# An adaLN block with attention and expert FFN on one core: split q, k and V kept in DRAM, later norms early, other work staggered

## The chip, the cores and the metric

The kernel runs on one core of a Trainium2 chip, in one launch. The metric is the device time in microseconds of that launch. Its engines have their own instruction queues: TensorE (PE; PEld is its weight loads), VectorE (DVE), ScalarE (ACT), GpSimd (POOL) and SyncE (SP), which only issues DMAs here.

## The reference

Four batches `x` of 1024 tokens with 256 features go through a modulated attention layer and a modulated FFN:

```python
mod = (_silu(c) @ wmod).reshape(4, 6, 1, -1)
sa, ca, ga, sb, cb, gb = (mod[:, i] for i in range(6))
ga = (2 * (ga >= 0) - 1) * maximum(abs(ga), 0.25)      # gb likewise
h = layernorm(x) * (1 + ca) + sa
x = x + ga * attn(h)          # 16 heads of 16 features, softmax over 1024 keys, projection with bias
h = layernorm(x) * (1 + cb) + sb
x = x + gb * ffn(h)
# ffn, for each batch on its own slices of the 1024 tokens:
base = h @ W_base + b_base
e = relu(h @ W_enc[n] + b_enc[n])                      # 8 autoencoders of width 64
recon = e @ W_dec[n] + b_dec[n]
loss[n] = mean((recon - h) ** 2);  top1 = argmin(loss)
out = base + relu(h @ W_down[top1] + b_down) @ W_up[top1] + b_up
```

All inputs and outputs are float32.

## The kernel before

**Attention.** A batch has four groups of four heads. For each group and each half of 512 queries, the main loop walks over 8 key tiles: 32 (batch, group, half) blocks of 8 steps, 256 steps, two steps to a turn of the loop. `begin` (L534) makes two score tiles `pt` per step on TensorE (L542: k times q, then a matmul that subtracts the row maxima by a mask `pick` and a row tile `mt`), each 128x1024, and ScalarE takes the exponential into `es` (L550). `weigh` (L502) adds the weighted values: four matmuls with `vaug`, V with columns of ones between (L506), so that the row sums come along.

The maxima are wanted before the scores of a group start. So `row_max` (L409) makes the scores once more, in the other orientation (`ps`, L448), a few groups ahead, and VectorE reduces them (L455). Per turn of two steps the loop emits four `pt` and about four `ps` tiles. `pt`, `ps` and the reconstruction tiles `pr` share one PSUM pool, `big`, of three buffers. When a group's maxima are done, `to_row` (L414) turns them on TensorE, copies them on VectorE, splits them on POOL with two instructions (`mrow`, L420 and L421), stores them to DRAM (L423) and loads them back into `mt` (L431).

q and k are split in two float32r parts each (high and low), so that one matmul gives float32 accuracy. `qk_chunk` (L326) makes the q or k of 128 features (two groups) of a batch in four tiles, ScalarE copies, POOL splits (L353, L354) into `qhl` and `khl`, one buffer each, in SBUF. `expand` (L393) copies the rows of two heads from there into 128-row tiles with four DMAs of 128 KB each (L402), two groups ahead. `v_all` (L362) makes V of a batch in four tiles and copies each into four of the five `vaug` buffers (L381): on ScalarE for batch 0, on VectorE later.

**Other work.** Beside the attention of batch b runs the preparation of batch b+1 (norm by `norm_first`, L301, then q, k, v) and `post(b-1)` (L556): projection, second norm, eight encoders in four pairs and two halves, reconstruction and its loss, the choice of the expert, the final matmuls. This work stands in lists, `Stream`s (L837), of items: `X` (instructions off TensorE or DMA), `D` (a TensorE tile with a weight; `FULL` is a whole one, 0.45 a turn of a norm half), `R` (one reconstruction tile, `decode`, L639: `pr` on TensorE, the difference `df` with one buffer on VectorE, L650, two squares with running sums on ScalarE, L655), and the controls `at`, `wait`, `need`, `done`, `take`, `give`, `by`. `fixed(b)` (L997) builds the lists of the preparation, and they start with the batch.

A turn of the loop (L1098) asks which lists are ready and picks a `PATTERN` (L1029) of the letters t (score tile), S (maxima), V (weighted sum), R. With reconstructions at the head of a list it takes two at once. `pressed` (L1114) is true when the sum of the lists' paces exceeds 0.6; then `dense` puts one more D tile in the turn.

**Order.** TensorE's order is that of the program. The other engines' and SyncE's orders come from a scheduler that plays the program with estimated costs; on the chip each engine then takes its instructions in that order. Ahead of the loop stands the prologue: weights, norm of batch 0, q/k of its first chunk, `expand` of two groups, then the maxima of group (0,0), and beside them the transposes of the remaining weights, V of batch 0 and `gate_rows` (L177): five POOL instructions (L192 to L196) and the store `gates` (L197). `post`'s first items, `load` (L560, two loads of x and one of the gates, `gt`) and `gate_proj` (L573, `wpg` and `gpb` on POOL), are ready early too.

A norm half (`norm_items`, L252) is: statistics of four tiles on VectorE (L260, L261), `ve` (L265), `rstd` on POOL (L267), four centrings on POOL (L272), then two turns on TensorE with a ScalarE copy (L284, L285). The tiles of x for it, `xin`, have three buffers, loaded by SyncE (`load_two`, L84); the centred half has the tag `half`, with three buffers shared with the encoders' results.

Of the kernel before, what the change touches and what calls it, by code (L numbers as in the profile page):

```python
# [26 lines left out]
def tile_adaln_block(  # L27
# [111 lines left out]

    def condition():  # L140
# [111 lines left out]
    def norm_items(src_of, dst_of, shift, scale, b, half, name, fast=False):  # L252
# [10 lines left out]
        def spread():  # L263
# [4 lines left out]
            s["xh"] = wa.tile([P, TH, D], F32, tag="half", name=f"xh_{name}", bufs=3)  # L268
# [27 lines left out]
        items += [("D", 0.45, [lambda c=c: turn(c)]) for c in range(NC)] + [("give", "half"), ("wait", 2)]  # L296
        return items
# [3 lines left out]
    def norm_first(b, between=()):  # L301
        def alloc():
            hT_of[b] = wa.tile([P, NC, S], F32, tag="hT", name=f"hT_{b}", bufs=1)

        items = [("X", alloc)]
        for half in range(NH):
            items += norm_items(
                lambda t, half=half: x_in[b, (half * TH + t) // 2][:, t % 2, :],
                lambda: hT_of[b],
                SA,  # L310
                CA,
                b,
                half,
                f"n1_{b}_{half}",
                b == 0,
            )
            if half == 0:
                items += between
        return items
# [6 lines left out]
    def qk_chunk(b, ch):  # L326
        def part(n, which, h, c, s={}):
# [17 lines left out]
            if c == NC - 1:  # L345
# [8 lines left out]
                nc.gpsimd.tensor_tensor(hl[:, 1, hs], fu, hl[:, 0, hs].bitcast(F32), ALU.subtract)  # L354

        return [
            ("D", FULL, [lambda n=n, w=w, h=h, c=c: part(n, w, h, c) for c in range(NC)])
            for n, w in enumerate("qk")
            for h in range(NH)
        ]  # L360

    def v_all(b):  # L362
        def part(u, t, s={}):
# [13 lines left out]
            if t == 1:  # L377
                copy = nc.vector.tensor_copy if b else nc.scalar.copy
                for g in range(NG):
                    va = vaug[(b * NG + g) % NV]  # L380
                    copy(  # L381
                        va[:, 2 * u : 2 * u + 2, :, 0::2],
                        pv[:, :, g * HG * HD : (g + 1) * HG * HD].rearrange(
                            "p t (j e) -> p t j e", e=HD
                        ),
                    )

        return [("D", FULL, [lambda u=u, t=t: part(u, t) for t in range(2)]) for u in range(NT // 2)]
# [4 lines left out]
    def expand(b, g, i):  # L393

        ch, r0 = g // GC, (g % GC) * HG * HD
        for which, order in (("q", (0, 0, 1, 1)), ("k", (0, 1, 0, 1))):
            hl = split[which, b, ch]
            t = wa.tile([P, S], F32R, tag=f"{which}64{i}", name=f"{which}64_{b}_{g}_{i}", bufs=3)
            r = slice(r0 + 2 * i * HD, r0 + (2 * i + 2) * HD)
            for n, part in sorted(enumerate(order), key=lambda x: x[1]):  # L400
                queue = nc.scalar if alone and which == "k" and g == 0 else nc.sync
                queue.dma_start(t[n::4, :].bitcast(F32), hl[r, part, :].bitcast(F32))  # L402
# [153 lines left out]
    def post(b, last=False):  # L556
# [64 lines left out]
        def encode(pr, h, c):  # L621
            hs = slice(h * HALF, (h + 1) * HALF)
            if c == 0:
                s["he", pr, h] = wa.tile([P, HALF], F32, tag="half", name=f"he_{b}_{pr}_{h}", bufs=3)
# [201 lines left out]

    groups = [(b, g) for b in range(B) for g in range(NG)]
# [7 lines left out]
    held = {"half": 3, "centre": 1}  # L835

    class Stream:  # L837
# [3 lines left out]
        def pace(self, step):  # L841

            most, due = 0.0, 0.0
            for item in self.items[self.at :]:
                if item[0] == "D":
                    due += item[1] * len(item[2]) / (2 * FULL)
# [4 lines left out]
            return most  # L851

# [49 lines left out]
    for g in range(2):  # L902
        for i in range(2):
            expand(0, g, i)
    mean_w = cst.tile([P, P], F32, name="mean_w")
# [27 lines left out]
    NV = NG + 1  # L933
# [63 lines left out]
    def fixed(b):  # L997

        moves, work = [], []
        k0 = b * BATCH  # L1000

        def moved(g, i):
            return ("X", lambda: expand(*groups[b * NG + g + 2], i))

        for g in range(NG):
            if b + 1 < B or g < NG - 2:
# [199 lines left out]
```

## Time and profile before

| | us |
|---|---|
| three timed runs: median (lowest, highest) | 1191.78 (1190.69, 1195.03) |
| the profiled execution | 1194.91 |
| its span | 1193.1 |
| mean granted TensorE clock | 0.978 of full |

Busy times by stage of that execution, from windows of the trace:

| stage | from, to (us) | length | PE busy | DVE | ACT | POOL | clock |
|---|---|---|---|---|---|---|---|
| up to the first exponential | 0.24, 80.0 | 79.76 | 46.52 | 42.66 | 13.77 | 26.13 | 0.84 |
| rest of group (0,0) | 80.0, 155.6 | 75.60 | 64.45 | 61.87 | 34.50 | 27.17 | 0.94 |
| rest of batch 0 | 155.6, 323.1 | 167.50 | 160.57 | 125.05 | 106.87 | 19.23 | 1.00 |
| batch 1 | 323.1, 597.8 | 274.70 | 260.31 | 192.59 | 170.77 | 62.27 | 1.00 |
| batch 2 | 597.8, 873.1 | 275.30 | 260.32 | 191.11 | 170.77 | 61.24 | 1.00 |
| batch 3 | 873.1, 1120.8 | 247.70 | 227.84 | 144.08 | 159.98 | 46.38 | 0.99 |
| tail | 1120.8, 1193.1 | 72.30 | 57.84 | 34.57 | 35.68 | 12.34 | 0.90 |

How to read the lines of the profile: "L542 PE MATMUL pt<-q,k" is TensorE's matmul of line 542 that writes pt and reads q and k; "x2048" is a count. In a group's line come busy us and mean ns of one, then the idle time of the engine ahead of these instructions and, after an arrow, the instruction that ended it. In the timeline a line starts with its start and length in us, and the bracket holds the idle time before it and its releaser. A float32 matmul leaves two records. The span's first instruction is at about 0.24 us in these windows.

### The profile page before, as it was taken

Reading aid. Unit: us, or ns where it says so; the run is one execution under the profiler, and the core shown is the slowest. Engines: PE = TensorE matmul, PEld = TensorE weight load, DVE = VectorE, ACT = ScalarE, POOL = GpSimd, SP = SyncE. Lnnn points to the kernel's source line nnn. Section 1 sums busy time; section 2 is a strip of 40 time slices with the busy share of each in tenths; the row PEclk is TensorE's granted clock in tenths of the full one; section 3 lists DMA queues with packets and bytes.
Section 4 is the critical chain, followed back from the end, with each engine's and each line's share of the span. In section 5 each row is a group of like instructions: output and inputs, shape, how many; then the busy total and the mean of one; then the engine's idle time right before and its main releaser. Section 6 shows DMA issues by size and latency. Waiting matters only on the chain.

```text
span 1193.1 us, 16436 instructions
## 1 busy us (share of the span) xinstructions
PE 1077.8 (90%) x6324; PEld 476.5 (40%) x6324; DVE 791.9 (66%) x975; ACT 692.3 (58%) x928; POOL 254.8 (21%) x271
## 2 busy tenths in 40 slices
PE   4768889999999889999999889999999889899995
PEld 3423333434444333345444333345444333344443
DVE  4477977777687666767678666676778777701264
ACT  2114466665666677654556667654655676647662
POOL 3155000200314002240224201140222200042003
PEclk9869999999999999999999999999999999999998
DMA  6522130122121201113131200204040300011001
GB/s 203 142 81 55 41 77 18 50 69 54 44 60 36 61 15 48 54 43 82 38 110 27 56 15 24 64 27 103 17 131 8 76 1 18 15 58 53 18 1 47
DMA packets 42582, 63.92 MB, mean 54 GB/s; under 512 B 13052, under 2 KB 28436, under 8 KB 42504
## 3 DMA queue, kind: packets, MB, share of 16 engines
q1 hardware_dynamic: 40000, 58.41, 18.2%
q10 hardware_dynamic: 1736, 3.15, 0.8%
q0 software_dynamic: 768, 1.31, 0.5%
q8 instruction: 50, 0.82, 0.3%
q14 instruction: 28, 0.23, 0.1%
HBM read 19.39 MB, written 5.19 MB: 21 GB/s over the span
## 4 chain that ended last, share of the span: by engine, by line
PE 69%; ACT 11%; DVE 10%; DMA 4%; issue 4%; POOL 2%; SPq 0%; ACTq 0%; DVEq 0%; POOLq 0%
PE pt L542 18%; PE pv L506 18%; PE ps L448 10%; ACT es L550 6%; DVE mx L455 5%; PE ph L626 4%; PE pr L647 3%; PE pq L338 3%; PE pvp L370 3%; ACT df L655 3%; DVE df L650 3%; PE ppj L591 2%; PE pf L761 2%; PE pk L338 2%; PE ptn_n L284 2%
## 5 line engine op out<-in xcount | busy, mean ns | idle before, releaser
L455 DVE TENSOR_REDUCE mx<-ps 128x2 f32<-128x1024 f32 x512 | 611.8, 1220 | 191.9 <-PE ps L448 188.2
L550 ACT ACTIVATE es<-pt 128x1024 f32<-128x1024 f32 x512 | 510.8, 1022 | 296.2 <-PE pt L542 289.5
L506 PE MATMUL pv<-es,vaug 128*32 128x512 f32 x2048 | 274.6, 607 | 0.1
L448 PE MATMUL ps<-k,q 64*128 64x512 f32 x1024 | 236.4, 461 | 35.0 <-ACT es L550 10.4
L542 PE MATMUL pt<-q,k 64*128 64x512 f32 x1024 | 239.0, 451 | 21.8 <-ACT es L550 10.7
L542 PE MATMUL pt<-mt,pick 64*128 64x512 f32 x1024 | 209.4, 393 | 4.6 <-DMA mt<-mdram 4.6
L448 PEld LDWEIGHTS ps<-k,q 64*128 64x128 f32 x1024 | 98.3, 186 | 201.4 <-issue 92.5
L542 PEld LDWEIGHTS pt<-q,k 64*128 64x128 f32 x1024 | 99.3, 184 | 170.7 <-DVE mx L455 96.8
L655 ACT ACTIVATE df<-df,fbias 128x512 f32<-128x512 f32 x128 | 91.1, 713 | 55.0 <-DVE df L650 55.0
L542 PEld LDWEIGHTS pt<-mt,pick 64*128 64x128 f32 x1024 | 100.4, 186 | 15.6 <-DMA mt<-mdram 5.8
L650 DVE TENSOR_TENSOR df<-pr,h2T 128x1024 f32<-128x1024 f32 x64 | 77.4, 1222 | 42.5 <-PE pr L647 20.7
L506 PEld LDWEIGHTS pv<-es,vaug 128*32 128x32 f32 x2048 | 40.5, 108 | 100.1 <-issue 90.8
L647 PE MATMUL pr<-he,wdec 64*128 64x512 f32 x256 | 64.3, 614 | 6.3 <-ACT es L550 6.2
L484 POOL TENSOR_TENSOR aT<-aT,su 128x512 f32<-128x512 f32 x14 | 17.8, 1273 | 238.9 <-DMA su<-rdram 189.5
L626 PE MATMUL ph<-h2T,wenc 128*128 128x512 f32 x128 | 63.6, 623 | 0.0
L781 DVE TENSOR_TENSOR x<-pf,x 128x512 f32<-128x512 f32 x16 | 10.8, 687 | 54.3 <-PE pf L772 22.1
L353 POOL CAST qhl<-fu_q 128x512 fp32r<-128x512 f32 x14 | 8.5, 610 | 178.4 <-ACT fu_q L352 175.9
L267 POOL TENSOR_TENSOR rstd_n<-ve_n,neghalf 128x4 f32<-128x4 f32 x16 | 16.8, 1048 | 102.2 <-DVE ve_n L265 96.4
L761 PE MATMUL pf<-wbg,h2T 128*128 128x256 f32 x128 | 37.4, 425 | 0.0
L647 PEld LDWEIGHTS pr<-he,wdec 64*128 64x128 f32 x256 | 21.6, 185 | 37.3 <-ACT es L550 13.2
L284 PE MATMUL ptn_n<-ident,xh_n 128*128 128x128 f32 x128 | 23.2, 311 | 14.0 <-ACT h2T L285 6.6
L626 PEld LDWEIGHTS ph<-h2T,wenc 128*128 128x128 f32 x128 | 22.3, 192 | 33.0 <-issue 31.8
(134 smaller groups left out, 755.8 us busy)
## 6 DMA issues: line engine op xcount, KB each, us to landing
q<-qhl SPq DMA_DIRECT2D x128, 128.0 KB
k<-khl SPq DMA_DIRECT2D x120, 128.0 KB
xin<-in_L_attn_x_dram SPq DMA_DIRECT2D x16, 256.0 KB
x<-in_L_attn_x_dram SPq DMA_DIRECT2D x8, 512.0 KB
aT<-ou SPq DMA_DIRECT2D x32, 128.0 KB
out_dram<-x SPq DMA_DIRECT2D x16, 256.0 KB
su<-rdram SPq DMA_DIRECT2D x14, 256.0 KB
wm<-in_L_wmod_dram ACTq DMA_DIRECT2D x1, 1024.0 KB
```

Source lines behind the costliest of these rows:

```text
L284: nc.tensor.transpose(pt[:, t, :], s["xh"][:, t, c * P : (c + 1) * P], ident)
L338: nc.tensor.matmul(pq, wqkv[:, c, n * D + ch * P : n * D + (ch + 1) * P], hT[:, c, hs], start=(c == 0), stop=(c == NC - 1),)
L448: nc.tensor.matmul(ps[:, a, :], q[r, t0 : t0 + P], k[r, h * HALF : (h + 1) * HALF], start=True, stop=True,)
L455: nc.vector.tensor_reduce(mx[:, h, hq, i::2, t], ps, AX.X, ALU.max, negate=True)
L506: nc.tensor.matmul(acc[h][j * STRIP : (j + 1) * STRIP, :], va[:, kt, j, :], es[j // 2][:, j % 2, :], start=(kt == 0), stop=(kt == NT - 1),)
L542: nc.tensor.matmul(pt[:, a, :], k[r, kt * P : (kt + 1) * P] if first else picks[i][r, :], q[r, hs] if first else mt[n % 2][r, hs], start=f ...
L550: nc.scalar.activation(e, pt, AF.Exp, scale=SCALE)
L626: nc.tensor.matmul(s["ph"], wenc[:, c, 2 * pr : 2 * pr + 2, :].rearrange("p n h -> p (n h)"), s["h2T"][:, c, hs], start=(c == 0), stop=(c ...
L647: nc.tensor.matmul(two[:, i, :], wdec[r, pr, c * P : (c + 1) * P], he[r, :], start=True, stop=True)
L650: nc.vector.tensor_tensor(df, two, h2T[:, c, hs].unsqueeze(1).to_broadcast([P, 2, HALF]), ALU.subtract)
L655: nc.scalar.activation(df[:, i, :], df[:, i, :], AF.Square, bias=bdec_of(e, c), accum_out=s["acc"][:, e, c, h : h + 1],)
L761: nc.tensor.matmul(po[u][:, t, :], s["h2T"][:, c, t0 : t0 + P], s["wbg"][:, c, :], start=(c == 0), stop=False,)
```

## The change

- `qk_chunk` stores each finished `qhl` and `khl` to DRAM three steps after its last tile (`hldram`), and `expand` reads from there with two DMAs of 256 KB per tile instead of four of 128 KB; only the first chunk of batch 0 is still read from SBUF. A chunk's tiles wait (`need`) until the other chunk's store has been issued.
- `v_all`: ScalarE copies each V tile into `vo` (one buffer), which is stored to DRAM (`vdram`). Batch 0 also fills `vaug` directly, three groups of it. `vaug` has three buffers instead of five, and `fetch_v` loads a group's values into `vi` and POOL spreads them into `vaug` four steps later.
- The norms of batches 1 to 3 stand in a list of their own from the start of the loop and run as buffers allow; their turns wait until the batch before is through with its q, k and V. `half` has four buffers. q, k and V of batches 1, 2 and 3 have the end steps of `AHEAD`; before, those of batch b+1 were spread over batch b.
- `post`'s six lists end 36, 28, 28, 18, 12 and 0 steps before the end of their batch instead of all at it.
- A turn takes one reconstruction instead of two when no list's `rate` asks for more than one per step.
- Reconstructions count 0.5 in `pace`, and `pressed` begins at 0.75.

```diff
+    hldram, vdram = {}, [dram.tile([P, NT, D], F32, name=f"vdram_{b}") for b in range(B)]
...
-            s["xh"] = wa.tile([P, TH, D], F32, tag="half", name=f"xh_{name}", bufs=3)
+            s["xh"] = wa.tile([P, TH, D], F32, tag="half", name=f"xh_{name}", bufs=4)
...
-    def norm_first(b, between=()):
...
+    def norm_first(b, load=None):
...
+        if b == 0:
+            return [("X", alloc)] + [item for centred, turns in both for item in centred + turns]
+        items = []
+        for half in range(NH):
+            for u in range(half * NT // 4, (half + 1) * NT // 4):
+                items.append(("X", lambda u=u: load(u)))
+            items += [("wait", 2)] + both[half][0]
+        items += [("need", ("free", b - 1)), ("X", alloc)]
+        return items + both[0][1] + both[1][1] + [("wait", 2), ("done", ("hT", b))]
...
     def qk_chunk(b, ch):
+        def store(which):
+            hl = split.pop((which, b, ch))
+            d = dram.tile([P, 2, S], F32, name=f"{which}dram_{b}_{ch}")
+            nc.sync.dma_start(d, hl.bitcast(F32))
+            hldram[which, b, ch] = d
+            done.add((which, b, ch))
...
+                if h == NH - 1:
+                    defer(3, lambda: store(which))
+
+        items = []
+        for n, w in enumerate("qk"):
+
+            items += [("need", (w, b - 1 + ch, 1 - ch))] if b + ch else []
+            items += [
+                ("D", FULL, [lambda n=n, w=w, h=h, c=c: part(n, w, h, c) for c in range(NC)])
+                for h in range(NH)
+            ]
+        return items
...
-                copy = nc.vector.tensor_copy if b else nc.scalar.copy
-                for g in range(NG):
-                    va = vaug[(b * NG + g) % NV]
-                    copy(
-                        va[:, 2 * u : 2 * u + 2, :, 0::2],
...
+                vo = wa.tile([P, 2, D], F32, tag="vo", name=f"vo_{b}_{u}", bufs=1)
+                nc.scalar.copy(vo, pv)
+                if b == 0:
+                    for g in range(NV):
+                        nc.scalar.copy(
+                            vaug[g][:, 2 * u : 2 * u + 2, :, 0::2],
...
+                def store():
+                    nc.sync.dma_start(vdram[b][:, 2 * u : 2 * u + 2, :], vo)
+                    done.add(("v", b, u))
...
+    def fetch_v(b, g):
+
+        vi = wa.tile([P, NT, HG * HD], F32, tag="vi", name=f"vi_{b}_{g}", bufs=1)
+        nc.sync.dma_start(vi, vdram[b][:, :, g * HG * HD : (g + 1) * HG * HD])
+
+        def spread():
+            nc.gpsimd.tensor_copy(
+                vaug[(b * NG + g) % NV][:, :, :, 0::2], vi.rearrange("p t (j e) -> p t j e", e=HD)
+            )
+
+        defer(4, spread)
...
-        for which, order in (("q", (0, 0, 1, 1)), ("k", (0, 1, 0, 1))):
-            hl = split[which, b, ch]
...
+        r = slice(r0 + 2 * i * HD, r0 + (2 * i + 2) * HD)
+        for which in "qk":
+            kept = (which, b, ch) in hldram
+            hl = hldram[which, b, ch][r] if kept else split[which, b, ch][r].bitcast(F32)
...
-                queue.dma_start(t[n::4, :].bitcast(F32), hl[r, part, :].bitcast(F32))
+                queue.dma_start(t[n::2].bitcast(F32), rows)
...
+    AHEAD = {1: (2 * STEPS, 3 * STEPS), 2: (4 * STEPS - 4, 4 * STEPS + 8), 3: (7 * STEPS, 9 * STEPS)}
...
-    held = {"half": 3, "centre": 1}
+    held = {"half": 4, "centre": 1}
...
-                if item[0] == "D":
-                    due += item[1] * len(item[2]) / (2 * FULL)
+                if item[0] in "DR":
+                    due += item[1] * len(item[2]) / (2 * FULL) if item[0] == "D" else 0.5
...
+        def rate(self, step):
+
+            n = sum(item[0] == "R" for item in self.items[self.at :])
+            return 2 * n / max(2, self.by - step) if self.by else 0
...
-    NV = NG + 1
+    NV = 3
...
-    def fixed(b):
...
+    def fetches():
+
+        moves = []
+        for n, (b, g) in enumerate(groups[2:]):
+            moves += [("at", n * STEPS + 1)] + [("need", (w, b, g // GC)) for w in "qk"]
+            moves += [("X", lambda b=b, g=g, i=i: expand(b, g, i)) for i in range(2)]
+            if n + 2 >= NV:
+                moves += [("need", ("v", b, NT // 2 - 1)), ("X", lambda b=b, g=g: fetch_v(b, g))]
+        return moves
+
+    def ahead():
+
+        norms, work = [], qk_chunk(0, 1) + [("by", 8), ("done", ("free", 0))]
+        for b in range(1, B):
+
+            def load(u, b=b):
+                x_in[b, u] = load_two(b, u)
+
+            norms += norm_first(b, load)
+            work += [("need", ("hT", b))] + qk_chunk(b, 0) + [("by", AHEAD[b][0])]
+            work += v_all(b) + qk_chunk(b, 1) + [("by", AHEAD[b][1]), ("done", ("free", b))]
+        return [norms, work]
...
-                streams += [Stream(items) for items in fixed(b)]
-                if b:
+                if b == 0:
+                    streams += [Stream(items) for items in [fetches()] + ahead()]
+                else:
                     end = k0 + BATCH - (STEPS + 2 if b == B - 1 else 0)
-                    streams += [Stream(items, end) for items in post(b - 1)]
+
+                    left = [36, 28, 28, 18, 12, 0]
+                    streams += [Stream(items, end - n) for items, n in zip(post(b - 1), left)]
...
-        kind = min(tiles, 1) * "D" + min(pairs, 2) * "R"
-        pressed = sum(s.pace(k0) for s in streams) > 0.6
+
+        pairs = min(pairs, 1 if all(s.rate(k0) <= 1 for s in streams) else 2)
+        kind = min(tiles, 1) * "D" + pairs * "R"
+        pressed = sum(s.pace(k0) for s in streams) > 0.75
```

## The prediction

> **What bounds the kernel now.** I read the page first: busy shares, chain, costliest groups.
>
> ```profile
> span 1193.1 us, 16436 instructions
> PE 1077.8 (90%) x6324; PEld 476.5 (40%) x6324; DVE 791.9 (66%) x975; ACT 692.3 (58%) x928; POOL 254.8 (21%) x271
> ...
> PE 69%; ACT 11%; DVE 10%; DMA 4%; issue 4%; POOL 2%; SPq 0%; ACTq 0%; DVEq 0%; POOLq 0%
> ...
> L455 DVE TENSOR_REDUCE mx<-ps 128x2 f32<-128x1024 f32 x512 | 611.8, 1220 | 191.9 <-PE ps L448 188.2
> L550 ACT ACTIVATE es<-pt 128x1024 f32<-128x1024 f32 x512 | 510.8, 1022 | 296.2 <-PE pt L542 289.5
> ```
>
> TensorE is busy 90% and leads the chain, yet 115 us of it stand idle. So a change is worth something in two places only: where TensorE's work shrinks or stops waiting, and before the main loop runs full. I therefore cut the span into windows: the time to the first exponential (prologue), the rest of group (0,0), the rest of batch 0, batches 1, 2, 3, and the tail. Columns: length, then busy us and count of PE, PEld, DVE, ACT, POOL, then TensorE clock, DMA share, GB/s.
>
> ```profile
> 0.24:80.00 79.76, 46.52 (x171) 27.52 (x172) 42.66 (x91) 13.77 (x36) 26.13 (x40) 0.84 0.53 149
> 80.00:155.60 75.60, 64.45 (x366) 25.08 (x362) 61.87 (x61) 34.50 (x36) 27.17 (x28) 0.94 0.20 52
> ...
> 597.80:873.10 275.30, 260.32 (x1567) 115.08 (x1566) 191.11 (x227) 170.77 (x225) 61.24 (x62) 1.00 0.19 50
> ```
>
> In batch 2 TensorE works 260 of 275 us; in the prologue 47 of 80. One turn of the main loop (two key tiles) costs, alone, with one q/k tile, with two reconstructions, and with two reconstructions and one encoder tile:
>
> ```profile
> 176.65:182.72 6.07, 5.72 (x44) 2.26 (x42) 4.84 (x5) 3.98 (x4) 0.00 (x0) 1.00 0.00 0
> 217.40:224.70 7.30, 7.30 (x47) 3.02 (x46) 5.16 (x5) 4.58 (x5) 3.17 (x3) 1.00 0.12 38
> 490.17:499.60 9.43, 7.56 (x49) 3.02 (x48) 5.99 (x6) 6.63 (x13) 0.00 (x0) 1.00 0.00 0
> 480.10:490.17 10.07, 9.58 (x54) 3.71 (x53) 7.09 (x6) 7.48 (x13) 4.87 (x5) 1.00 0.34 90
> ```
>
> The pair adds 3.36 us with only 1.84 us of TensorE work in it. The timeline of that turn shows why: there is one df buffer, so the second subtraction waits for the squares of the first, and the score tile behind it waits for its PSUM buffer.
>
> ```profile
> 496.07 1.23 DVE L650 TENSOR_TENSOR df<-pr,h2T 128x1024 f32<-128x1024 f32 x1 [1.59 <-ACT df L655]
> ...
> 497.35 0.50 PE L448 MATMUL ps<-k,q 64*128 64x512 f32 x2 [1.45 <-DVE df L650]
> ```
>
> **The change, part 1: where D tiles stand.** TensorE's order, compared instruction by instruction, gives per turn the number of full tiles (q/k, v, projection, encoder), turn items and reconstructions. A first full tile costs 7.30 - 6.07 = 1.23, two cost 3.21 (turns with two took 9.28 in the same trace), a turn item's pair of transposes 2.3 (turns of 8.4). Reconstruction pairs cost 3.36 alone, 2.77 beside one tile (10.07 - 7.30), 2.3 beside two (11.6 - 9.28).
>
> Batch 0 (after its first group): 5 more turns with a tile, +6.2; one norm half more to turn, +4.6; together +10.8. Batch 1: before, 16 turns with one tile and 4 with two (19.7 + 12.8), pairs 2 alone, 4 beside one, 2 beside two (6.7 + 11.1 + 4.6), sum 54.9; after, 11 with one, 10 with two (13.5 + 32.1), sixteen single reconstructions, of which 2 alone, 10 beside one tile, 4 beside two. Batch 2: before 54.9 again; after 12 with one tile (14.8), none with two, sixteen singles (9 alone, 7 beside one), one norm half fewer to turn (-4.6). Batch 3 keeps most pairs but puts tiles together: 40.0 against 37.6, +2.4. The tail's order is the same but for one encoder.
>
> **Part 2: a single reconstruction.** No row shows one. From above it costs half a pair: 1.68 alone, 1.38 beside one tile, 1.15 beside two. From below, nothing alone (VectorE has 1.23 us free in a plain turn, and one subtraction takes 1.22) and its own TensorE time beside tiles, where TensorE is already full: the L647 rows give 64.3 / 64 = 1.00. I take 0.95 alone (a plain turn sends 8 PSUM tiles through 3 buffers in 6.07; 9 would take 6.83, and its df still waits a little), 1.0 beside one, 1.2 beside two. The singles then cost 16.7 in batch 1 and 15.6 in batch 2. Batch 1: 13.5 + 32.1 + 16.7 - 54.9 = +7.4. Batch 2: 14.8 + 15.6 - 4.6 - 54.9 = -29.1. Main loop: 10.8 + 7.4 - 29.1 + 2.4 = -8.5, call it **-9**; with the bounds -20 (singles at 0 + 17 + 4 instead of 32) to +6 (47).
>
> **Part 3: V and split q, k through DRAM.** VectorE loses 48 copies of 283 ns (13.6 us), ScalarE gets 16 copies of about 0.59 (its fu copy), POOL 13 spreads near 1.2, SyncE 30-odd more issues, the DMA engines some 21 MB on top of 63.92, so their 20% becomes 27%. TensorE hides all this: the same full turns have 2 us free on VectorE and 2.7 on ScalarE. Without cover the ScalarE copies are 9 us. Stores that wait on SyncE for POOL's split replace loads that waited there for the same split. I take 0, bounds 0 and +3.
>
> **Part 4: norms of batches 1 to 3 start early, and this is where I expect the loss.** In the changed order POOL does, after batch 1's first half as before, also the centring of n1_1_1 and n1_2_0 *ahead of* the five gate instructions, then wpg *between* the two mrow instructions, then rstd, gpb and four centrings of n1_2_1. SyncE carries xin_3_1 and xin_3_2 (whose buffers those centrings free) ahead of the two mt loads that the first exponential needs. All this issues in order. Before:
>
> ```profile
> 62.90 1.93 POOL L192 TENSOR_SCALAR sg<-ga 4x512 f32<-4x512 f32 x1 [23.87 <-ACT ga L190]
> ...
> 73.43 0.45 POOL L421 TENSOR_TENSOR mrow<-mfull,mrow 32x128 fp32r<-32x128 f32 x1
> ...
> 75.37 1.40 SPq L431 DMA_DIRECT2D mt<-mdram  x2
> ...
> 80.00 1.02 ACT L550 ACTIVATE es<-pt 128x1024 f32<-128x1024 f32 x1 [15.39 <-PE pt L542]
> 80.81 4.84 POOL L272 TENSOR_SCALAR xh_n<-xin,mv_n,rstd_n 128x256 f32<-128x256 f32 x4
> 85.62 1.29 POOL L577 TENSOR_TENSOR wpg<-wproj,gt 128x512 f32<-128x512 f32 x1
> ```
>
> The chain after: VectorE's sixth maximum ends at 55.4, n1_1_1's statistics at 57.0, rstd 1.04 and centrings 4.84 on POOL to 63.0. The load of xin_2_1 waits for the first two (60.6), lands after 2.2 more; the seventh maximum stands behind it in VectorE's queue. n1_2_0's variances come at 67.9, its rstd and centrings end at 73.9, the gates (62.90 to 70.66 before, 7.76 long) at 81.7. Then gates' store, two loads of x, the load of gt: 82 to 84 issued, landed about 88. wpg 1.29 and mrow 0.45: 89.7 where it was 73.88. rstd, gpb 0.73 and four centrings: 96.4. Only then xin_3_2, and mt issues at 96.8 instead of 75.37; 4.63 later (as before) the first exponential, at 101 instead of 80.0. Shorter landings of gt and mt would make it 99. From that +19 to +21 I take back 3: norm waits that stood in the following stretch (1.80 us for xin at 85.8, and TensorE's 2 us behind it) were paid already. Net **+17**; the bounds are +21, nothing recovered, and +9, if the maxima don't wait (the gates then start at about 70 and end near 78) and 3 to 7 us come back in the first group.
>
> TensorE's clock belongs to this: the profile grants 0.67 to 0.68 from 62.9 to 89.3 around the wait, and four q/k matmuls took 3.53 us at 89.33 against 1.98 at 100.52. I count nothing for it, since the slow restart merely moves to the new start. [...]
>
> **Sum.** -9 + 0 + 17 = +8 on the profiled 1194.91 (span 1193.1 and 1.8 around it), so 1203; that run stood 3.1 over the median, so 1200 against 1191.78.
>
> **Rivals.** *A, faster: the start costs nothing.* Place: POOL and SyncE before the first exponential. If the early norms fit into gaps (POOL idles 23.87 us before 62.90, and that speaks for it) the main loop's -9 stands alone: 1183. It decides from a prologue loss under 3 us, 9 less the 6 that 0.5% is. Against: wpg and xin_3_2 stand ahead of mrow and mt whatever the gaps hold. *B, it cancels:* singles cost only their TensorE time, -20 + 17 = -3: 1189. For: TensorE's 5.72 of 6.07. Against: the df row's ScalarE wait. *C, a single costs half a pair*, so splitting saves nothing: +6 + 17 = +23, 1215. For: each still puts VectorE 1.22 and ScalarE 1.8 into one turn. Against: the 1.59 us wait comes only with a second. *That it doesn't do what it says* is excluded for the order: thirty-two turns of batches 1 and 2 carry one reconstruction in the changed program.
>
> **How the numbers follow.** Forecast 0.40, A 0.23, B 0.22, C 0.15. The likeliest is 1200. A measurement here tells about 0.5% (6 us) from no change: slower is over 1197.7, faster under 1185.8. Forecast and C give slower but for the forecast's low edge: 0.51. A gives faster but for a small part, and B a little: 0.26. The rest, 0.23, is within. The range takes in half of A's spread and nearly all of C: 1183 to 1214.
>
> **What would show it.** The first exponential at 99 to 101 with mt as its releaser; POOL's second mrow right behind wpg; TensorE idle 15 us or more before it. Turns with one reconstruction near 7.0, or 8.3 beside a tile, and no subtraction waiting for L655's squares in batches 1 and 2. Batch 2 near 246, batch 1 near 282. It is wrong if the first exponential comes before 90, or if batches 1 and 2 together are not 15 to 30 shorter.

## The result, and the profile after

The changed kernel takes 1204.17 us (median of 6 runs, 1201.03 to 1207.29), the kernel before, measured beside it, 1193.4 (1189.54 to 1199.05). The ratio is 1.0083, 95% interval 1.0061 to 1.0105: it is slower, by 0.8%. The forecast was 1200 against 1191.78.

The page of the changed kernel: span, busy time, the chain that ended last, and the two groups shown of before.

```profile
span 1202.8 us, 16378 instructions
...
PE 1073.3 (89%) x6324; PEld 476.9 (40%) x6324; DVE 782.1 (65%) x927; ACT 701.2 (58%) x940; POOL 261.6 (22%) x282
...
PE 67%; DVE 13%; ACT 7%; issue 4%; DMA 4%; POOL 3%; SPq 1%; ACTq 0%; DVEq 0%; POOLq 0%
...
L511 DVE TENSOR_REDUCE mx<-ps 128x2 f32<-128x1024 f32 x512 | 610.8, 1220 | 217.2 <-PE ps L504 212.5
L606 ACT ACTIVATE es<-pt 128x1024 f32<-128x1024 f32 x512 | 510.3, 1021 | 275.7 <-PE pt L598 262.1
```

TensorE does 4.5 us less than before, and the span is 9.7 us longer: what was lost is waiting. Where it was lost, windows tell (length, busy us and count of PE, PEld, DVE, ACT, POOL, TensorE clock, DMA share, GB/s; here the start, the rest of group (0,0), batches 1 and 2):

```profile
0.24:103.70 103.46, 46.80 (x171) 27.44 (x172) 47.66 (x116) 14.93 (x36) 47.85 (x58) 0.77 0.53 145
103.70:178.00 74.30, 64.46 (x369) 25.30 (x367) 61.48 (x60) 35.46 (x38) 10.54 (x14) 0.95 0.19 68
...
357.50:635.40 277.90, 269.65 (x1606) 122.80 (x1606) 187.81 (x203) 177.13 (x237) 60.80 (x65) 1.00 0.23 79
635.40:881.80 246.40, 235.77 (x1486) 102.50 (x1486) 186.46 (x203) 163.56 (x215) 43.03 (x45) 1.00 0.19 61
```

In the table a stage begins with the first exponential of its first step (before's batches 1 to 3: 324.0, 598.7, 874.0), and the last stage with the last exponential.

| stage | before | after | difference | forecast |
|---|---|---|---|---|
| start, to the first exponential | 80.0 | 103.7 | +23.7 | +19 to +21 |
| rest of group (0,0) | 76.6 | 74.3 | -2.3 | -3 |
| rest of batch 0 | 167.4 | 179.5 | +12.1 | +10.8 |
| batch 1 | 274.7 | 277.9 | +3.2 | +7.4 |
| batch 2 | 275.3 | 246.4 | -28.9 | -29.1 |
| batch 3, to the last exponential | 250.7 | 251.7 | +1.0 | +2.4 |
| tail | 68.4 | 69.3 | +0.9 | 0 |

So the largest loss stands ahead of the first exponential; the +12.1 of batch 0 is work moved there, near the forecast. Timelines of the changed kernel there (start, length, engine and instruction, in brackets the idle time before and what ended it), POOL first:

```profile
70.78 4.83 POOL L274 TENSOR_SCALAR xh_n<-xin,mv_n,rstd_n 128x256 f32<-128x256 f32 x4
75.58 1.93 POOL L194 TENSOR_SCALAR sg<-ga 4x512 f32<-4x512 f32 x1
...
84.92 0.28 POOL L476 CAST mrow<-mfull 32x128 fp32r<-32x128 f32 x1 [1.57 <-DVE mfull L474]
91.14 1.26 POOL L633 TENSOR_TENSOR wpg<-wproj,gt 128x512 f32<-128x512 f32 x1 [5.94 <-DMA gt<-gates]
92.36 0.44 POOL L477 TENSOR_TENSOR mrow<-mfull,mrow 32x128 fp32r<-32x128 f32 x1
...
94.49 4.83 POOL L274 TENSOR_SCALAR xh_n<-xin,mv_n,rstd_n 128x256 f32<-128x256 f32 x4
```

The gates (sg) follow the centring of n1_2_0 without a gap, 12.7 later than before's 62.90. Their input came hardly sooner: ScalarE copied ga only at 73.77 (before at 62.24). Its copy of the fourth tile of V had waited 7.62 us for the store of the third, and TensorE (pg, from which ga is copied) had waited 6.34 for ScalarE. SyncE, ScalarE and TensorE:

```profile
62.84 2.77 SPq L90 DMA_DIRECT2D xin<-in_L_attn_x_dram  x2
65.71 4.25 SPq L417 DMA_DIRECT2D vdram<-vo  x2
```

```profile
69.00 0.58 ACT L406 COPY vo<-pvp 128x512 f32<-128x512 f32 x1 [7.62 <-DMA vdram<-vo]
```

```profile
70.16 3.57 PE L184 MATMUL pg<-wm,cs 128*4 128x256 f32 x8 [6.34 <-ACT vaug L409]
```

That store stood on SyncE behind two loads of xin, whose buffers n1_1_1's centrings (60.40 to 65.22) free. The maxima that follow pg on TensorE were late with it: VectorE took up the last eight that mrow needs at 74.39 instead of 62.68. Between the two halves of mrow POOL stands 5.94 us idle for gt, which only wpg needs. Later on SyncE's queue, and on TensorE:

```profile
92.83 0.35 SPq L479 DMA_DIRECT2D mdram<-mrow  x1
96.95 2.78 SPq L90 DMA_DIRECT2D xin<-in_L_attn_x_dram  x2
99.82 1.40 SPq L487 DMA_DIRECT2D mt<-mdram  x2
```

```profile
102.35 1.22 PE L598 MATMUL pt<-mt,pick 64*128 64x512 f32 x2 [13.84 <-DMA mt<-mdram]
```

The two xin loads wait for buffers that the centrings of 94.49 free, and mt stands behind them; TensorE waits 13.84.

### The profile page after: what moved, and what is told of

It reads as the page before. It is cut to its first block, busy times and chain, and to the rows that moved or that the text cites. A ratio compares the mean times of both kernels' runs of the same rounds, so it can differ in the third digit from the quotient of the medians.

```text
span 1202.8 us, 16378 instructions
## 1 busy us (share of the span) xinstructions
PE 1073.3 (89%) x6324; PEld 476.9 (40%) x6324; DVE 782.1 (65%) x927; ACT 701.2 (58%) x940; POOL 261.6 (22%) x282
## 2 busy tenths in 40 slices
DMA packets 58375, 86.20 MB, mean 72 GB/s; under 512 B 25005, under 2 KB 40389, under 8 KB 56505
## 4 chain that ended last, share of the span: by engine, by line
PE 67%; DVE 13%; ACT 7%; issue 4%; DMA 4%; POOL 3%; SPq 1%; ACTq 0%; DVEq 0%; POOLq 0%
PE pt L598 18%; PE pv L562 18%; PE ps L504 10%; DVE mx L511 8%; PE ph L682 5%; ACT es L606 4%; PE pr L703 3%; DVE df L706 3%; PE ppj L647 2%; PE pq L359 2%; PE pf L817 2%; PE pk L359 2%; PE pvp L397 2%; ACT df L711 2%; POOL xh_n L274 2%
## 5 line engine op out<-in xcount | busy, mean ns | idle before, releaser
L598 PE MATMUL pt<-q,k 64*128 64x512 f32 x1024 | 234.5, 442 | 20.2 <-DVE mx L511 9.2
L598 PEld LDWEIGHTS pt<-mt,pick 64*128 64x128 f32 x1024 | 101.0, 186 | 25.8 <-DMA mt<-mdram 14.3
L269 POOL TENSOR_TENSOR rstd_n<-ve_n,neghalf 128x4 f32<-128x4 f32 x16 | 16.7, 1045 | 103.8 <-DVE ve_n L267 99.3
L837 DVE TENSOR_TENSOR x<-pf,x 128x512 f32<-128x512 f32 x16 | 10.8, 687 | 42.9 <-PE pf L828 23.7
L437 POOL COPY vaug<-vi 128x512 f32<-128x512 f32 x13 | 8.5, 652 | 130.2 <-PE pv L562 106.4
L476 POOL CAST mrow<-mfull 32x128 fp32r<-32x128 f32 x17 | 4.8, 280 | 142.3 <-DVE mfull L474 142.3
L690 ACT ACTIVATE he<-ph,fbias 128x512 f32<-128x512 f32 x32 | 21.9, 685 | 23.1 <-PE ph L682 23.1
```

Of the source, the lines that this page charges most:

```text
L598: nc.tensor.matmul(pt[:, a, :], k[r, kt * P : (kt + 1) * P] if first else picks[i][r, :], q[r, hs] if first else mt[n % 2][r, hs], start=f ...
```

## Experiments

Each edit is to the changed kernel. A "hold" is a tiny POOL instruction that writes one column of a tile from a mark, which POOL wrote from the first exponential of a named step; the load or statistics that use the tile then come after it. In the code, "..." marks lines left out. Starts of exponentials in us, by step (step 16 ends group (0,0), 64 begins batch 1, 128 batch 2, 192 batch 3):

| run | step 0 | 8 | 16 | 24 | 48 | 64 | 128 | 192 | span |
|---|---|---|---|---|---|---|---|---|---|
| before | 80.0 | 125.1 | 156.6 | 183.6 | 264.0 | 324.0 | 598.7 | 874.0 | 1193.1 |
| changed | 103.7 | 146.5 | 178.0 | 210.7 | 298.3 | 357.5 | 635.4 | 881.8 | 1202.8 |
| e1 | 96.5 | 139.0 | 170.4 | | 290.9 | 349.9 | 628.1 | 874.0 | 1194.1 |
| e2 | 99.2 | 148.3 | 179.8 | | 300.1 | 359.1 | 638.9 | 886.9 | 1207.6 |
| e3 | 95.7 | 138.2 | 169.6 | | 290.0 | 349.2 | 628.7 | 877.0 | 1197.4 |
| e4 | 87.3 | 130.6 | 172.6 | 211.0 | 298.6 | 357.8 | 636.0 | 884.6 | 1205.2 |
| e5 | 83.3 | 132.4 | 166.8 | 204.9 | 292.6 | 351.6 | 629.9 | 875.8 | 1196.6 |
| e6 | 105.1 | 147.7 | 179.2 | 211.8 | 299.6 | 358.7 | 647.8 | 897.6 | 1219.1 |
| e7 | 103.7 | 146.2 | 177.7 | 210.1 | 297.5 | 356.9 | 634.6 | 880.6 | 1200.6 |
| e8 | 93.8 | 147.0 | 178.4 | 210.8 | 298.5 | 357.7 | 635.8 | 883.2 | 1203.9 |
| e9 | 83.6 | 126.4 | 160.7 | 195.0 | 289.7 | 348.7 | 628.5 | 874.6 | 1194.6 |
| e10 | 80.3 | 122.0 | 154.9 | 187.2 | 286.2 | 345.5 | 624.1 | 872.1 | 1192.5 |
| e11 | 77.9 | 120.4 | 151.9 | 184.1 | 272.9 | 332.0 | 613.1 | 859.4 | 1180.1 |

### e1, e2, e3: taking single links out of the chain

The mark is written in `begin` after the first exponential. e1 holds gt of `post(0)` by it, e2 the loads xin_3_1 and xin_3_2 in `load_two`, e3 both.

```diff
             nc.scalar.activation(e, pt, AF.Exp, scale=SCALE)
+            if not begun:
+                begun.append(True)
+                nc.gpsimd.tensor_scalar(begin_t, e[:, 0, :1], 0.0, 0.0, ALU.mult, ALU.add)
...
+            if b == 0:
+                nc.gpsimd.tensor_copy(s["gt"][:, 0, :1], begin_t)
             nc.sync.dma_start(s["gt"], gates[b].partition_broadcast(P))
...
+            if (b, u) in {(3, 1), (3, 2)}:
+                nc.gpsimd.tensor_copy(xt[:, 0, :1], begin_t)
```

> Changed kernel, with the load of gt for batch 0 (and so wpg, gpb and the four additions to x) held until the first exponential. Theory of the queue order (mrow stands behind wpg on POOL): the second mrow instruction follows the first at once, at 85.3 instead of 92.36, the centrings of n1_2_1 end at 91.4 instead of 99.3, mt is issued at 92 to 93 instead of 99.82 and the first exponential comes at 95 to 97 instead of 103.5, about 7.5 earlier. Rival (the early traffic and POOL's amount of work set the start, whatever the order): the same instructions are still to be done, the first exponential moves by under 2.

Measured: 1195.84 in one run (before 1194.52 beside it, changed 1204.17). The first exponential came at 96.5, and the 7.2 us won are still there at the end (span 1194.1). POOL in e1:

```profile
85.48 0.28 POOL L477 CAST mrow<-mfull 32x128 fp32r<-32x128 f32 x1 [1.69 <-DVE mfull L475]
85.84 0.45 POOL L478 TENSOR_TENSOR mrow<-mfull,mrow 32x128 fp32r<-32x128 f32 x1
86.26 1.03 POOL L270 TENSOR_TENSOR rstd_n<-ve_n,neghalf 128x4 f32<-128x4 f32 x1
```

With gt held the 5.94 us between the two mrow instructions are gone. No work was taken away, only its place; the rival that only the amount counts falls.

> Changed kernel, with the loads xin_3_1 and xin_3_2 held until the first exponential, so that they stand behind mt on SyncE. Queue order: mrow stays at 92.4 to 92.8, mt is issued 1.3 after mdram's store, at 94.5 instead of 99.82, first exponential at 98 to 99, 5 earlier. Rival (mt waits for traffic): under 2 earlier, since only two of the loads move.

Measured: 1209.79 in one run; mt issued at 95.26, first exponential 99.2, each within 1 of what was expected, 4.5 earlier. But by step 8 that was lost again and 1.8 more: VectorE had batch 3's statistics in its queue ahead of maxima, and waited 5.17 us for the held load (issued at 105.64). TensorE waited 4.07 for VectorE, and its granted clock was 0.50 over the six us behind that (111.1 to 117.1).

> Both holds together. Queue order: mrow at 85.3, mt issued at 87.4 instead of 99.82, first exponential at 91 to 92, 12 earlier, more than either alone as both stand in one chain; what is left over before's 80.0 is the centrings ahead of the gates and the maxima behind n1_1_1's and n1_2_0's statistics, 11 to 12. Rival: at most the sum of two small gains, 3.

Measured: 1199.23 in one run; first exponential 95.7, four later than expected. mrow came at 86.93 and mdram's store at 87.40, but SyncE in e3 issued mt only here:

```profile
87.40 0.35 SPq L482 DMA_DIRECT2D mdram<-mrow  x1
91.75 1.38 SPq L490 DMA_DIRECT2D mt<-mdram  x2
```

mt waits for the store to land. Before the change 1.46 lay between the two issues (73.91 and 75.37), here 4.35, with two loads of x of 512 KB issued ahead at 86.02. So a third link had hidden behind the two. That these loads hold the store up is an inference until e5.

### e4, e5: all later norms after the start

e4 holds xin_1_3 by a mark of step 0 and the four loads of batch 2 by one of step 8. e5 holds loads and, by later marks, the tiles bs of the statistics (`marks` below stands for a table of half and mark); its steps (load/statistics) are n1_1_1 0/2, n1_2_0 5/7, n1_2_1 9/11, n1_3_0 13/15, n1_3_1 17/19, and 0 for x and gt of `post(0)`.

```diff
+            if name in marks:
+                nc.gpsimd.tensor_copy(bs[:, :1], token[marks[name]])
             nc.vector.bn_stats(bs, src_of(t))
```

> Changed kernel, with the load xin_1_3 held until the first exponential and the loads of x of batch 2 until the first exponential of step 8, so that all norms but the first half of batch 1 stand behind the start. Queue order: first exponential at 80 to 81, 23 earlier than the changed kernel's 103.5; later stages as in the changed kernel (batch 0 after its first group +12 against before, batch 1 +3, batch 2 -29, batch 3 +1), total 1180 to 1186, ratio to before 0.989 to 0.995. Rival (the main loop's gain hangs on the early norms, or the start on the traffic): 1196 or more, ratio 1.00 or above.

Measured: 1206.41, ratio 1.0102 (1.0079 to 1.0126). The expectation failed: the first exponential came at 87.3 (mdram 78.67, mt 83.35, the loads of x and gt ahead of it), and the 16 us won at the start were gone by step 24. In e4, VectorE and then TensorE at the end of group (0,0):

```profile
165.19 0.43 DVE L265 BATCH_NORM_STATS2 bs_n<-xin 128x6 f32<-128x256 f32 x1 [6.60 <-DMA xin<-in_L_attn_x_dram]
```

```profile
166.80 0.79 PE L601 MATMUL pt<-q,k 64*128 64x512 f32 x2 [6.00 <-DVE mx L514]
```

The same wait as at the start, at another place: statistics stand in VectorE's queue ahead of maxima, and their data is not there. Behind it TensorE ran three us at a clock of 0.50 and three at 0.62. The rival's number came true; e5 was to tell whether the early norms pay for something or only stand badly.

> Changed kernel; the loads of x and gt of post(0) and xin_1_3 wait for the first exponential, and from there each later norm half has its loads held to one step and its statistics to a step two later (steps 0/2, 5/7, 9/11, 13/15, 17/19), so that no statistics stand in VectorE's queue ahead of data that is still on its way. Queue order: first exponential at 79 to 81 (before 80.0, changed 103.7); mt's wait for mdram, 4.4 to 4.7 in the two runs with x's loads ahead of it, falls to 1.5; group (0,0) ends at 155 to 158 where the run with held loads alone had lost 10; from there the changed kernel's own course (+12 to the end of batch 0, then +3, -29, +1): total 1180 to 1186. Rival (the early norms pay for the main loop, so what the start gains is given back whatever the order): group (0,0) or the next two lose 10 or more again, total 1195 to 1206.

Measured: 1202.53 (4 runs, 1198.39 to 1204.22), ratio 1.007 (1.0048 to 1.0092). With x's loads behind it mt follows mdram by 1.47:

```profile
77.91 0.33 SPq L485 DMA_DIRECT2D mdram<-mrow  x1
79.38 1.39 SPq L493 DMA_DIRECT2D mt<-mdram  x2
```

In e2, where the loads of x and gt had been issued 7 us and more ahead of mdram, it was 1.47 too (93.79 to 95.26). So loads issued just ahead were the third link. The first exponential is 3.3 from before. But steps 0 to 8 took 49.1 (changed 42.8): a statistic waited 4.41 on VectorE for POOL's mark, and TensorE 3.74 for the maxima behind it. Steps 16 to 24 took 38.1 (changed 32.7): around step 16 statistics waited 2.39 and 2.33 for their loads, TensorE 1.93 for mt and 3.60 for VectorE. The total missed its expectation and lay in the rival's range; whether the norms' place or their amount costs this was still open.

### e6, e7: the main loop

```diff
-pairs = min(pairs, 1 if all(s.rate(k0) <= 1 for s in streams) else 2)
+pairs = min(pairs, 2)
```

> Changed kernel with reconstructions always in pairs; pace, limits and lists as changed. By the terms of the prediction for a single (0.95 alone, 1.0 beside one tile, 1.2 beside two) against a pair (3.36, 2.77, 2.3) batches 1 and 2 become 12 longer together, by the turns measured in the changed kernel (7.36 - 6.07, 8.14 - 7.30, 10.06 - 9.21) also about 12: total 1213 to 1217. Rival (a single costs half a pair): no change, 1204.

Measured: 1221.27 in one run; batches 1 and 2 took 289.1 and 249.8, 14.6 more than the changed kernel's. That is 0.9 for each of the 16 pairs, a little more than expected; that a single costs half a pair is excluded. The two batches share it unevenly, 11.2 and 3.4, which was not taken apart. The subtraction's group in e6 and then in the changed kernel (busy, mean ns, idle before by releaser):

```profile
L706 DVE TENSOR_TENSOR df<-pr,h2T 128x1024 f32<-128x1024 f32 x64 | 77.3, 1223 | 40.9 <-PE pr L703 20.9 <-ACT df L711 16.0 <-issue 2.4
```

```profile
L706 DVE TENSOR_TENSOR df<-pr,h2T 128x1024 f32<-128x1024 f32 x64 | 77.3, 1222 | 21.5 <-PE pr L703 13.1 <-ACT df L711 6.0 <-issue 2.2
```

The wait for the squares (ACT df) falls from 16.0 to 6.0. All of the 6.0 stand in batch 3, where pairs remain; in batches 1 and 2 no subtraction waits for squares, as the prediction said.

```diff
             nc.sync.dma_start(d, hl.bitcast(F32))
+            d2 = dram.tile([P, 2, S], F32, name=f"{which}twice_{b}_{ch}")
+            nc.sync.dma_start(d2, hl.bitcast(F32))
...
                     nc.sync.dma_start(vdram[b][:, 2 * u : 2 * u + 2, :], vo)
+                    if b:
+                        v2 = dram.tile([P, 2, D], F32, name=f"vtwice_{b}_{u}")
+                        nc.sync.dma_start(v2, vo)
```

> Changed kernel with every store of split q and k, and every store of V of batches 1 to 3, issued twice, the second into a tile that nobody reads: 17 MB more written. If the way through DRAM is hidden, as the prediction has it: 0 to +3, 1203 to 1208, all stages within 1. Rival (the traffic and the issues on SyncE are part of the loss): +5 or more, in the batches where the stores are.

Measured: 1202.36 in one run, every stage within 1 of the changed kernel's. 104.01 MB were moved instead of 86.20. So the stores of q, k and V in the loop are hidden; the loads from DRAM and POOL's spreads were not doubled.

### e8 to e11: the norms by need

In e8 vo of batch 0 holds eight key tiles of 64 columns and is stored once, after the last.

```diff
-                nc.scalar.copy(vo, pv)
+                if b == 0:
...
+                    nc.scalar.copy(vo[:, 2 * u : 2 * u + 2, :], pv[:, :, NV * HG * HD :])
+                else:
...
+                    nc.scalar.copy(vo, pv)
...
+                    if b == 0 and u == NT // 2 - 1:
+                        nc.sync.dma_start(vdram[b][:, :, NV * HG * HD :], vo)
```

> Changed kernel; in batch 0 ScalarE copies only the values of the fourth group (the only ones fetched from DRAM) into one tile of all eight key tiles, stored once, so that no copy waits for a store. What is tested is whether the wait for vo, 5.25 and 1.96 in the changed kernel, is part of the late start. Queue order: ga again at about 62, the gates at 63 to 71, ahead of n1_1_1; mrow behind wpg (gt lands at about 78) at 79 to 81, mt behind n1_1_1's centrings (xin_2_1 and xin_2_2 stand ahead of it) at 85 to 87, first exponential at 89 to 91 instead of 103.7. Rival (vo's wait is hidden, maxima set the pace): gates and first exponential as in the changed kernel, within 2.

The expectation names two of the waits for vo; the third is the 7.62 shown above.

Measured: 1205.8 in one run. ga was copied at 64.84 instead of 73.77, the gates started at 65.50, now ahead of n1_1_1's centrings in POOL's order, and mrow's second half came at 84.21 behind wpg (gt had landed by 81.05); first exponential 93.8. Gates and first exponential came later than expected by 3. The 10 us gained were lost again by step 8: TensorE waited 4.05 and 3.68 for VectorE, and ran at a clock of 0.50 (105.1 to 108.0) and 0.66 (108.0 to 111.0) behind the first. So the wait for vo was a link of its own in the late start, and taking it away alone moves the loss on. How much is the wait and how much POOL's new order, e8 does not tell.

e9 is e8 with holds as in e5, at other steps, and the list of the norms is tied to about the same steps by `at`. e10 moves them again, holds two of a half's four statistics, and expands the first chunk from SBUF by four DMAs as the kernel before. e11 moves batch 3's and x's. The steps (load/statistics) are the whole edit from e10 to e11:

| | n1_1_1 | n1_2_0 | n1_2_1 | n1_3_0 | n1_3_1 | x, gt |
|---|---|---|---|---|---|---|
| e9 | 0/2 | 18/20 | 22/24 | 27/29 | 33/35 | 11 |
| e10 | 0/3 | 18/21 | 24/27 | 30/34 | 36/40 | 44 |
| e11 | 0/3 | 18/21 | 24/27 | 36/40 | 43/47 | 9 |

```diff
-            if name in marks:
+            if t % 2 == 0 and name in marks:
                 nc.gpsimd.tensor_copy(bs[:, :1], token[marks[name]])
...
+                if not kept:
+                    break
...
+            if not kept:
+                order = (0, 0, 1, 1) if which == "q" else (0, 1, 0, 1)
+                for n, part in sorted(enumerate(order), key=lambda x: x[1]):
+                    queue = nc.scalar if alone and which == "k" and g == 0 else nc.sync
+                    queue.dma_start(t[n::4, :].bitcast(F32), hl[:, part, :])
```

> e8 with the norms spread by need: n1_1_1 loaded at the first exponential with statistics at step 2, x and gt of post(0) at step 11, the halves of batch 2 loaded at steps 18 and 22, of batch 3 at 27 and 33, their statistics two steps later. Queue order: first exponential at 79 to 81, end of group (0,0) at 154 to 157 (before 156.6), steps 16 to 24 within 1 of the changed kernel's 32.7 (e5 38.1), then the changed kernel's course: total 1178 to 1184, ratio to before 0.988 to 0.993. Rival (early norms pay for the main loop): what the start gains is lost by step 48, 1195 or more.

Measured: 1192.04 (12 runs, 1190.86 to 1196.87), ratio 0.9985 (0.9973 to 0.9998). In the profiled execution, 1196.41, the first exponential came at 83.6, TensorE waited 1.89 for mt ahead of step 16, steps 16 to 24 took 34.3, and waits were left at steps 32 to 40 (a statistic 2.13 for its load, TensorE 2.96 for VectorE), which took 32.3 for the changed kernel's 26.8. So the sum was missed.

> e9 with what its trace still showed waiting taken away: only two of the four statistics of a half wait for the mark (the pool of bs has three buffers, so the fourth mark waited for an aggregate, 1 to 3 each time), statistics stand three or four steps behind their loads, x and gt of post(0) come at step 44 instead of 11 (their additions stood ahead of the mrow of group (0,1)), and the first chunk is expanded from SBUF by four DMAs of 128 KB again. Queue order: first exponential at 79 to 81 (e9 83.6), step 16 at 154 to 156 (e9 160.7), step 48 at 281 to 284 (e9 289.7, before 264.0, changed 298.3), from there the changed kernel's course; total 1178 to 1184, ratio to before 0.987 to 0.993. Rival (the norms cost this time wherever they stand): within 3 of e9, ratio 0.996 to 1.0.

Measured: 1192.6 (12 runs, 1187.13 to 1194.66), ratio 0.9977 (0.9963 to 0.9991). The start was as expected (80.3, and 154.9 at step 16), step 48 not (286.2): steps 32 to 48 took 68.7 in the profiled execution, 1194.29. Two waits stand in that stretch. In e10, VectorE:

```profile
229.91 0.35 DVE L550 RECIPROCAL rs<-rs 128x32 f32<-128x32 f32 x1 [3.07 <-DMA rs<-sdram]
```

and TensorE, with the windows over that stretch (the clock is the third number from the end):

```profile
232.11 0.80 PE L621 MATMUL pt<-q,k 64*128 64x512 f32 x2 [3.57 <-DVE mx L534]
...
281.59 0.50 PE L527 MATMUL ps<-k,q 64*128 64x512 f32 x2 [2.74 <-ACT es L629]
```

```profile
232.00:235.00 3.00, 2.89 (x12) 1.75 (x12) 2.93 (x8) 1.31 (x2) 0.84 (x1) 0.50 0.15 41
235.00:238.00 3.00, 3.00 (x14) 0.70 (x12) 1.43 (x2) 1.76 (x2) 2.89 (x4) 0.50 0.15 58
```

The second wait came from POOL, which waited 5.38 for gt; then wpg, gpb and two of the four additions to x stood ahead of the end of a split of batch 1's q. ScalarE waited 5.54 for that buffer, and TensorE for ScalarE.

> e10 with only times moved: x and gt of post(0) at step 9 instead of 44 (there POOL's 7 us for them stood ahead of the split of batch 1's q, and TensorE waited 2.74 and ran at half clock after it), batch 3's halves loaded at steps 36 and 43 instead of 30 and 36, statistics four steps later (at 34 they met a late load of rs on VectorE, and TensorE waited 3.57 and then ran six us at half clock). Queue order: steps 32 to 48 take 59 as in the changed kernel (e10 68.7), step 48 of the program at 274 to 277; the rest as e10: total 1180 to 1186, ratio to before 0.988 to 0.994. Rival (the waits come back elsewhere): within 3 of e10, ratio 0.995 to 1.0.

Measured: 1182.15 (4 runs, 1180.86 to 1183.67), ratio to before 0.9899 (0.9882 to 0.9915): 1.0% faster than the kernel before, and 22 us below the changed kernel. Steps 32 to 48 took 58.7. The page, POOL, SyncE and ScalarE of e11, for the place where the changed kernel lost:

```profile
span 1180.1 us, 16424 instructions
...
PE 1075.7 (91%) x6324; PEld 478.0 (41%) x6324; DVE 781.6 (66%) x927; ACT 700.7 (59%) x940; POOL 267.4 (23%) x315
```

```profile
71.75 0.28 POOL L499 CAST mrow<-mfull 32x128 fp32r<-32x128 f32 x1 [2.41 <-DVE mfull L497]
72.12 0.45 POOL L500 TENSOR_TENSOR mrow<-mfull,mrow 32x128 fp32r<-32x128 f32 x1
```

```profile
72.60 0.34 SPq L502 DMA_DIRECT2D mdram<-mrow  x1
73.03 0.58 SPq L450 DMA_DIRECT2D vi<-vdram  x1
74.06 1.39 SPq L510 DMA_DIRECT2D mt<-mdram  x2
```

```profile
77.94 1.02 ACT L629 ACTIVATE es<-pt 128x1024 f32<-128x1024 f32 x1 [14.65 <-PE pt L621]
```

TensorE is as busy as before to 2.1 us (1075.7 and 1077.8), and the span is 13 us shorter. It keeps the changed lists, singles and DRAM copies and adds 33 small POOL instructions; apart from the places it differs from the changed kernel in V of batch 0 (one store) and the first chunk's expand (four DMAs). The rival that the norms cost this time wherever they stand is out: only the places differ between e10 and e11. e9 to e11 change several places at once, so what each single hold is worth was not measured.

## Why the prediction was right

**The start: right in the links that it names, incomplete, and 3 to 5 too short in size.** Each named link is in the trace: gates behind n1_2_0's centring (75.58; the chain said 73.9), mrow behind wpg (92.36; 89.7), mt behind xin_3_2 (99.82; 96.8), first exponential 103.7 (101). TensorE idled 13.84 ahead of it, where 15 or more was named as a sign. The chain ran about 2 late from its first link on (the sixth maximum ended at 57.25; 55.4), and gt's landing, put at 88, was 91.14. Most of the 2 is a term that the prediction put at nothing: the first chunk's tiles came later by two DMAs of 256 KB than by four of 128 KB. TensorE's first score tile for the maxima, in the kernel before, then in the changed one:

```profile
42.47 0.80 PE L448 MATMUL ps<-k,q 64*128 64x512 f32 x2 [7.91 <-DMA q<-qhl]
```

```profile
44.12 0.79 PE L504 MATMUL ps<-k,q 64*128 64x512 f32 x2 [10.06 <-DMA k<-khl]
```

In all ten runs with two DMAs (the changed kernel, e1 to e9) it came at 44.1 to 46.1, in the three with four (before, e10, e11) at 42.5 to 43.0. e1 to e5 show that the links set the start: taking out wpg gives 7.2, all of them together 20.4 (e5). What the chain had not seen is the third link, mdram's store behind x's loads; in the changed kernel it is covered by the other two.

That POOL takes its instructions in order, which the chain rests on, e1 and the changed kernel show for mrow: its second half followed the first at once in the one (85.48, 85.84) and stood behind wpg in the other (84.92, 92.36). TensorE's clock, for which nothing was counted, was 0.95 over the rest of group (0,0) and 0.94 before.

The forecast took back 3 us in the following stretch; 2.3 came back. The net of start and group (0,0) was +21.4, not +17, just over the bound of +21.

**The loop: right to 4 us, some of it by errors that cancel.** The last four stages gave -12.6 and the tail +0.9, together -11.7, where -9 was put. Single reconstructions were to cost 0.95 alone, 1.0 beside a tile, 1.2 beside two. Windows over three such turns of the changed kernel (beside two, beside one, alone):

```profile
438.19:448.26 10.07, 10.07 (x53) 4.08 (x52) 6.03 (x5) 6.76 (x10) 0.00 (x0) 1.00 0.08 19
498.89:507.03 8.14, 8.14 (x50) 3.39 (x49) 6.03 (x5) 6.08 (x9) 0.00 (x0) 1.00 0.40 126
787.55:794.91 7.36, 6.83 (x44) 2.66 (x44) 5.93 (x6) 5.91 (x10) 0.00 (x0) 1.00 0.06 21
```

Against 9.21 (a turn with two tiles in the changed kernel; the four from 367.3 to 404.2 took 9.14 to 9.29), 7.30 and 6.07 without one that is 0.86, 0.84 and 1.29. Over 4, 17 and 11 turns: 3.4 + 14.3 + 14.2 = 31.9, where 32.3 were put. Beside tiles a single is cheaper than its TensorE time in the group's rows suggested, alone it is dearer: VectorE is busy 5.93 of 7.36 there, and TensorE idles 0.53. Batch 2 came out at -28.9 for -29.1; batch 1 at +3.2 for +7.4, of which the cheaper singles beside tiles explain 2.3 (14.4 for 16.7); the rest was not taken apart.

**The sum: partly luck.** The start was 4.4 worse than put and the loop 2.7 better. So the total came out at +9.7 on the profiled executions, where +8 was put, closer than either part.

**The way through DRAM** was taken as hidden. In the loop its stores are (e7); a spread on POOL took 0.65, where 1.2 was put. In the prologue it isn't: ScalarE's copies into vo waited 5.25, 1.96 and 7.62 for the store of the tile before, a wait that the prediction's part 3 didn't list. Through TensorE it made ga and the last maxima 11 to 12 late. So two paths lead to the late gates in the changed kernel, and they end 1.2 us apart: ga is copied by 74.34, the centrings end at 75.58. e8 takes the wait for vo away and wins 9.9 at the start; e5 leaves vo as it is, holds the later norms and wins 20.4. In e5 the wait of 7.62 falls to 1.94, since the store has no loads of xin ahead of it on SyncE. So the place of the norms is the larger part of the loss, and some of it acts by way of vo; the two were not separated further.

**The rivals.** A (the start costs nothing) fell by its own mark, a prologue loss under 3: mrow and mt stood behind wpg and xin_3_2, and it was 23.7. With the start mended the loop's gain does stand alone, as A had it: 1183 there, 1182.15 in e11. B wanted singles at their TensorE time, -20; C half a pair each, +6; the loop gave -11.7, between B and the forecast, and e6 excludes C.

## What to carry to other kernels

When work is moved ahead, list for each in-order queue what it now stands in front of, DMA queues too, and follow the last of those waits to the engine that sets the end; a resource that is 22% busy (POOL in the changed kernel) can still be the one that is late. Early work with slack should be tied to the step that needs it, not to the moment when its buffers are free: holding the same norms off the start gave back 20 us (e5), loaded together inside group (0,0) they cost 11 there (e4), and spread to where each queue had room they cost at most about 3 in a batch against the changed kernel (e11). A wait taken away can uncover the next (in e3 mdram's 4.35, in e8 TensorE's 4.05), so look at the start of several later steps, not only at the place that was mended.

## What the runs showed of the hardware

Some short waits of TensorE cost more than themselves. In e10 one of 3.57 us was followed by six us at a granted clock of 0.50, in which pairs of matmuls that take 0.40 a little later took 0.63. In e9 one of 1.89 (for mt, ended at 159.28) was enough; the clock was 1.00 up to that wait, and behind it:

```profile
159.30:162.30 3.00, 3.00 (x12) 1.62 (x16) 1.23 (x1) 1.35 (x2) 0.00 (x0) 0.50 0.25 67
162.30:165.30 3.00, 3.00 (x16) 1.16 (x8) 0.79 (x1) 1.28 (x2) 0.68 (x1) 0.50 0.92 309
```

Shorter ones differ: a wait of 1.70 in the tail was followed by three us at 0.72 in the changed kernel and at 1.00 in e1, and the waits of 1.45 in the pair turns of before left the clock at 1.00.

mdram's store of 16 KB was slower to be seen behind large loads. It let the next load of its data go after 1.46 or 1.47 us where no load had been issued in the 2.8 us ahead (before, e2, e5, e11). It took 4.35 with two loads of 512 KB issued in the two us ahead (e3), and 4.68 with the same two and gt's (e4).
